# A third accumulating fold of the key totals, and a stack half as wide, in an attention kernel

## The chip, the cores and the metric

The kernel runs on one core of one Trainium2 chip. The metric is the device time of one execution in microseconds (us). Before the change it is 1807.54 us, the median of three runs (1806.34 to 1808.13).

## The reference

The input is 32 images of 256 channels on 32x32 pixels, in float32. Each image is group-normalized (32 groups of 8 channels), then goes through a causal self-attention with 8 heads of 32 dimensions over 1024 tokens, and the input is added to the output. A token attends only to tokens strictly before it:

```python
q = jnp.einsum('oc,bcs->bos', q_w, xf) + q_b[None, :, None]
kv = jnp.einsum('oc,bcs->bos', kv_w, xf) + kv_b[None, :, None]
...
mask = jnp.tril(jnp.ones((S, S), dtype=x.dtype), -int(MASK_CENTER))
scores = jnp.einsum('bhqd,bhkd->bhqk', q, k) / jnp.sqrt(jnp.asarray(dk, x.dtype))
scores = jnp.where(mask == 0, jnp.asarray(-10000.0, x.dtype), scores)
attn = jax.nn.softmax(scores, axis=-1)
attn = jnp.where(mask == 0, jnp.asarray(0.0, x.dtype), attn)
out = jnp.einsum('bhqk,bhkd->bhqd', attn, v)
...
x = x + _L0_conv_ref(_gn(x), q_w, q_b, kv_w, kv_b)
```

## The kernel before, in words

**Visits.** An image's attention is done in ten visits: two groups of four heads (g = 0, 1), and for each of them five visits (i = 0 to 4) that cover the lower triangle of keys by queries. In a visit TensorE makes transposed scores (keys on the partitions, queries along the row) for four heads: full blocks into two PSUM tiles `sT`, and triangular and odd pieces into one tile `tri`. ScalarE (ACT) takes their exponentials into SBUF tiles: `e` (128 keys x 4 heads x 512 queries) and `eh`. GpSimd (POOL) masks the triangular parts (`select`, L388), in place or into tiles `diagonal`. TensorE multiplies the exponentials with the values into a bank `acc`. The loop at L820 runs over all visits of all images; in its iteration i it writes down the scores of visit i, the values of visit i-1, and whatever the tables `at` and `after` hold for i. That fixes every engine's order by hand: five engines each work through their own list strictly in order, SyncE (SP) too, which issues most transfers.

**Key totals.** The softmax's denominators are sums of exponentials over all keys. VectorE (DVE) adds the visits' tiles together elementwise (`add_keys`, L490), so each image leaves four sums (two head groups by two query halves; n = 0 to 3 in the code), each a tile of 128 partitions x 4 heads x 512 queries, which still has to be summed over its 128 partitions. This is done by transfers: `fold` (L505) lets POOL issue an accumulating transfer that adds rows 64 to 127 onto rows 0 to 63 of the same tile, then another that adds rows 32 to 63 onto rows 0 to 31. Then `stack` (L511) lets SP copy the remaining 32 rows of each sum into 32 rows of one tile `folded`, so that the four sums lie above each other. `sum_folded` (L518, L519) transposes `folded` in 32x32 blocks, a head at a time, and reduces over the 32 keys: four transposes and four reductions per image, written into `rows`. `invert` (L547 to L559) checks the range, takes reciprocals and sends them to DRAM; `spread_inverses` (L573) reads them back, broadcast over 32 partitions each, into `rb`. `finish` (L598 to L607) multiplies, adds bias and input, and sends the output.

**The order around the change.** Sum n of image b is folded first at iteration first + SUMS[n] and second one iteration later; it is stacked at first + STACK[n], where first is the image's first visit. Both folds stand in POOL's list among the masks of the running visits; a fold waits there for the one before it to land, and POOL does nothing else meanwhile. The first fold of sum 1 also waits for a semaphore `begun`, which ACT raises at visit 7. In the same list stand, once an image, the gather of normalization statistics (`eight`, L212) and the small operations `rstd` and `shift` (L250, L254), for which ACT waits when it normalizes the next image (`xn`, L269). In SP's list a stack waits for the fold to land; `with_scores` (L568) holds some other issues until a given visit's scores have been made. The exponentials of visit 0 and 1 of each head group are written over the tiles of the same sums of the image before (four buffers `e0`), so they wait for those stacks.

The last image sums over keys on TensorE instead. The very first value projection, at the head of the program, uses the second half of a PSUM tile whose first half holds a projection of k.

Of the kernel before, what the change touches and what calls it, by code (L numbers as in the profile page):

```python
# [17 lines left out]
P = 128  # L18
# [10 lines left out]
ROW = 64  # L29
KEYS = 64  # L30
# [3 lines left out]
def tile_norm_attention_residual(  # L34
# [69 lines left out]
    def unshifted():  # L104
# [197 lines left out]
        def projections(b):  # L302

            def qk(n, g, hf, *bank):
                return lambda: project_qk(b, g, n, hf, *bank)

            def v(n, *bank):
                return lambda: project_v(b, n, *bank)

            early = [lone] if b == 0 else []  # L310
            return [
                qk(0, 0, 0, *early), qk(1, 0, 0), qk(0, 0, 1, *early), v(0), qk(1, 0, 1), qk(0, 1, 0, lone),
                qk(1, 1, 0), v(1), v(2), v(3), qk(0, 1, 1), qk(1, 1, 1, lone),
            ]
# [192 lines left out]
        def stack(b, n):  # L507
            if n == 0:
                live["folded", b] = work.tile([P, 4, HALF], F32, tag="folded", bufs=1, name=f"folded_{b}")
            total = live.pop(("sum", b, *divmod(n, NH)))  # L510
            nc.sync.dma_start(out=live["folded", b][n * HD : (n + 1) * HD], in_=total[:HD])  # L511

        def sum_folded(b, heads):
            if heads.start == 0:
                live["rows", b] = small.tile([P, ROW], F32, tag="rows", name=f"rows_{b}")
            for j in heads:
                turned = small.tile([P, HALF], F32, tag="turned", bufs=1, name=f"turned_{b}_{j}")
                nc.vector.transpose(turned, live["folded", b][:, j, :])  # L518
                nc.vector.tensor_reduce(  # L519
                    live["rows", b][:, j * HALF // HD : (j + 1) * HALF // HD],  # L520
                    turned.rearrange("p (k r) -> p k r", r=HD), AX.X, ALU.add,
                )
# [55 lines left out]
        def invert_here(b, n, within=slice(0, HALF)):  # L578


            if ("rb", b) not in live:
                live["rb", b] = work.tile([P, 4, HALF], F32, tag="folded", bufs=1, name="rb_last")
# [140 lines left out]
        STACK = (6, 9, 11, 14)  # L723
# [6 lines left out]
        with tc.manual_schedule(engines={ENG.PE, ENG.Activation, ENG.DVE, ENG.Pool, ENG.SP}):  # L730
# [14 lines left out]
            odd = work.tile([P, 4, HALF], F32, tag="folded", bufs=1, name="less_mean")[:, 0, :]  # L745
# [32 lines left out]
            for b in range(B):  # L778
# [14 lines left out]
                if not last:  # L793
                    for n in every:
# [3 lines left out]
                        when(first + STACK[n], lambda b=b, n=n: stack(b, n), at if n else after)  # L798
                    late = b == B - 2
                    v = first + N + (4 if late else 5)  # L800
# [215 lines left out]
```

## Time and profile before

| | us |
|---|---|
| median of the runs | 1807.54 |
| the profiled execution, its own time | 1806.47 |
| its span, from the first to the last instruction | 1803.3 |
| TensorE matmuls (PE) busy | 1782.8 |
| DVE busy | 1682.6 |
| ACT busy | 1469.8 |
| POOL busy | 833.2 |

The granted TensorE clock was 0.999 of full speed on average. A row of the timeline gives the start in us from the span's start, the duration in us, the engine, the line of the kernel, the operation, the tiles written and read, shapes and how many were merged into the row, and in brackets the idle time of the engine before it and what is thought to have ended it. A row of the waits gives engine and line, what was waited for, the total in us, how often, and the longest. A row of the transfers gives what is written and read, the issuing queue, the count, the size, and the median time from issue to landing in us. "Busy" of PE says that a matmul was under way, not that it ran at its best. The issue of a transfer on POOL is shown as an instruction of about 0.8 us; its landing comes later.

### The profile page before, as it was taken

Reading aid. Unit: us, or ns where it says so; the run is one execution under the profiler, and the core shown is the slowest. Engines: PE = TensorE matmul, PEld = TensorE weight load, DVE = VectorE, ACT = ScalarE, POOL = GpSimd, SP = SyncE. Lnnn points to the kernel's source line nnn. Section 1 sums busy time; section 2 is a strip of 40 time slices with the busy share of each in tenths; the row PEclk is TensorE's granted clock in tenths of the full one; section 3 lists DMA queues with packets and bytes.
Section 4 is the critical chain, followed back from the end, with each engine's and each line's share of the span. In section 5 each row is a group of like instructions: output and inputs, shape, how many; then the busy total and the mean of one; then the engine's idle time right before and its main releaser. Section 6 shows DMA issues by size and latency. Waiting matters only on the chain.

```text
span 1803.3 us, 82014 instructions
## 1 busy us (share of the span) xinstructions
PE 1782.8 (99%) x37208; PEld 983.7 (55%) x37208; DVE 1682.6 (93%) x1852; ACT 1469.8 (82%) x1736; POOL 833.2 (46%) x935
## 2 busy tenths in 40 slices
PE   8999999999999999999999999999999999999998
PEld 5555555555555555555555555555555555555554
DVE  3789999999999999999999999999999999999996
ACT  5888888888888888888888888888888888888884
POOL 2445644444444444544544444545444444445541
PEclk9999999999999999999999999999999999999999
DMA  2566776666766767767667666676676676666662
GB/s 69 105 118 129 150 134 137 137 138 136 149 127 138 144 134 148 129 134 143 131 145 146 129 137 142 137 148 128 136 147 131 145 143 131 138 140 136 131 120 86
DMA packets 92771, 240.23 MB, mean 133 GB/s; under 512 B 26272, under 2 KB 27792, under 8 KB 76544
## 3 DMA queue, kind: packets, MB, share of 16 engines
q0 software_dynamic: 17360, 100.58, 39.0%
q1 hardware_dynamic: 74912, 134.28, 26.3%
q8 instruction: 292, 4.78, 1.1%
q14 instruction: 63, 0.52, 0.1%
q10 hardware_dynamic: 144, 0.07, 0.0%
HBM read 69.90 MB, written 34.95 MB: 58 GB/s over the span
## 4 chain that ended last, share of the span: by engine, by line
PE 57%; DVE 32%; issue 5%; DMA 3%; ACT 2%; DVEq 0%; SPq 0%; POOL 0%; ACTq 0%
DVE e L490 20%; PE acc L472 17%; PE pp L180 14%; PE tri L381 10%; PE sT L381 8%; PE ppv L180 7%; DVE turned L518 3%; DVE rows L519 3%; DVE rb L601 2%; DMA rb<-inverses 2%; DVE num L598 2%; ACT eh L446 2%; DVE st L196 1%; PE pd L526 1%; DVE mv L219 1%
## 5 line engine op out<-in xcount | busy, mean ns | idle before, releaser
L443 ACT ACTIVATE e<-sT 128x1024 f32<-128x1024 f32 x640 | 620.8, 1022 | 209.1 <-PE sT L381 204.3
L381 PE MATMUL tri<-q,k 32*64 32x128 f32 (+4 forms) x12416 | 550.4, 298 | 8.8 <-ACT eh L446 8.1
L381 PE MATMUL sT<-q,k 32*64 32x256 f32 (+1 forms) x7424 | 548.7, 462 | 1.2 <-issue 1.2
L381 PEld LDWEIGHTS tri<-q,k 32*64 32x64 f32 x12416 | 389.0, 131 | 185.9 <-issue 86.6
L388 POOL TENSOR_SCALAR_AFFINE_SELECT diagonal<-eh 128x512 f32<-128x512 f32 x384 | 363.2, 966 | 265.6 <-ACT eh L446 265.3
L180 PE MATMUL pp<-xn,wT 128*32 128x512 f32 (+1 forms) x4224 | 477.5, 582 | 0.0
L490 DVE TENSOR_TENSOR e<-e,eh 128x1536 f32<-128x1536 f32 x375 | 438.3, 1169 | 41.5 <-PE acc L472 28.2
L446 ACT ACTIVATE eh<-tri 128x1536 f32<-128x1536 f32 (+1 forms) x320 | 453.2, 1416 | 23.6 <-DVE e L490 23.6
L490 DVE TENSOR_TENSOR e<-e,e 128x2048 f32<-128x2048 f32 x187 | 447.4, 2393 | 6.4
L505 POOL DMA_DIRECT2D e<-e x248 | 206.5, 833 | 414.9 <-DMA e<-e 360.9
L472 PE MATMUL acc<-e,v 128*32 128x512 f32 x2560 | 338.5, 600 | 1.1 <-POOL diagonal L388 1.1
L381 PEld LDWEIGHTS sT<-q,k 32*64 32x64 f32 x7424 | 301.1, 131 | 15.2 <-issue 1.9
L180 PEld LDWEIGHTS pp<-xn,wT 128*32 128x32 f32 x4224 | 140.5, 109 | 270.6 <-issue 216.2
L490 DVE TENSOR_TENSOR e<-e,diagonal 128x1024 f32<-128x1024 f32 x187 | 245.0, 1310 | 19.4
L180 PE MATMUL ppv<-wT,xn 128*32 128x256 f32 x4032 | 240.6, 379 | 0.0
L472 PE MATMUL acc<-eh,v 128*32 128x384 f32 (+3 forms) x3072 | 198.7, 346 | 0.0
L472 PEld LDWEIGHTS acc<-eh,v 128*32 128x32 f32 x3072 | 97.0, 110 | 143.1 <-issue 120.6
L180 PEld LDWEIGHTS ppv<-wT,xn 128*32 128x32 f32 x4032 | 129.7, 110 | 69.0
L388 POOL TENSOR_SCALAR_AFFINE_SELECT e<-e 128x512 f32<-128x512 f32 x64 | 73.2, 1144 | 196.1 <-ACT e L443 196.1
L269 ACT ACTIVATE xn<-x,shift,rstd 128x256 f32<-128x256 f32 x248 | 135.4, 594 | 8.8 <-POOL shift L254 8.4
L601 DVE SCALAR_TENSOR_TENSOR rb<-num,v_bias_col,x 128x256 f32<-128x256 f32 x248 | 131.3, 569 | 4.4
L472 PEld LDWEIGHTS acc<-e,v 128*32 128x32 f32 x2560 | 62.8, 108 | 105.2 <-issue 94.6
(94 smaller groups left out, 1267.9 us busy)
## 6 DMA issues: line engine op xcount, KB each, us to landing
e<-e POOLq DMA_DIRECT2D x124, 512.0 KB, 6.2
x<-in_x_dram SPq DMA_DIRECT2D x124, 256.0 KB, 4.1
e<-e POOLq DMA_DIRECT2D x124, 256.0 KB, 4.7
folded<-e SPq DMA_DIRECT2D x124, 256.0 KB, 4.5
rb<-inverses SPq DMA_DIRECT2D x124, 256.0 KB, 5.0
out_dram<-rb SPq DMA_DIRECT2D x124, 256.0 KB, 3.8
x<-in_x_dram SPq DMA_DIRECT2D x2, 512.0 KB, 5.8
inverses<-inv_turned SPq DMA_DIRECT2D x31, 32.0 KB, 2.9
```

What stands on the lines that cost most here:

```text
L180: nc.tensor.matmul(out[part, cols], lhsT=lhsT[:, part], rhs=rhs[:, cols], start=start, stop=stop, skip_group_check=True)
L269: nc.scalar.activation(to, of, AF.Identity, bias=live["shift", b][:, g : g + 1], scale=rstd)
L381: return nc.tensor.matmul(to[c : c + KEYS, at : at + width], lhsT=live["k", b, g][rows, kb * P + c : kb * P + c + KEYS], rhs=live["q", b, ...
L388: nc.gpsimd.affine_select(out=to, in_=of, pattern=[[0, 4], [(1, -1)[odd], P]], compare_op=ALU.is_gt, fill=0.0, base=0, channel_multiplier= ...
L443: nc.scalar.activation(e[:, heads[a][0] : heads[a][1] + 1 : step, :], banks[a], AF.Exp)
L446: exp = nc.scalar.activation(eh[:, :, :wide], tri.rearrange("p (j q) -> p j q", q=SHORT)[:, :, :wide], AF.Exp)
L472: nc.tensor.matmul(acc[HD * j : HD * (j + 1), of], lhsT=live["v", b][:, kb, h * HD : (h + 1) * HD], rhs=e[:, j, :], start=first, stop=last ...
L490: nc.vector.tensor_add(to, to, tile_of(b, g, at))
L505: nc.gpsimd.dma_start(out=total[:rows], in_=total[rows : 2 * rows], accum_op=ALU.add)
L518: nc.vector.transpose(turned, live["folded", b][:, j, :])
L519: nc.vector.tensor_reduce(live["rows", b][:, j * HALF // HD : (j + 1) * HALF // HD], turned.rearrange("p (k r) -> p k r", r=HD), AX.X, ALU ...
L601: nc.vector.scalar_tensor_tensor(blocks(rb, s), blocks(num, s, (start + s) % 2 == 1), v_bias_col[:, g : g + 1], blocks(xt[:, g, cols], s), ...
```

## The change

- **A third fold.** After the two folds, POOL issues a third accumulating transfer for each sum, which adds rows 16 to 31 onto rows 0 to 15. It stands one iteration after the second fold (SUMS[n] + 2).
- **A narrower stack.** The 16 rows that remain are stacked by two transfers, one for each half of the 512 queries, one under the other: `folded` becomes 128 partitions x 4 heads x 256 queries. Rows n·32 to n·32+15 hold the first half of sum n's queries, the next 16 rows the second half.
- **Half the operations on DVE.** `sum_folded` transposes two heads at once (2 x 256 columns) and reduces over 16 keys and not 32: two transposes and two reductions per image.
- **Places.** The stack of sum 0 moves from iteration 6 to 7, and to the end of the iteration. For the last but one image the sums over keys come one iteration later than before, as for the others.
- **Tiles.** Two tiles that shared the buffer of `folded` at the head and the end of the program go elsewhere or are taken as a slice of the smaller one.
- **The head.** The first value projection of image 0 uses the spare bank of the value products (`lone`).

```diff
+TURN = 16
...
-                qk(0, 0, 0, *early), qk(1, 0, 0), qk(0, 0, 1, *early), v(0), qk(1, 0, 1), qk(0, 1, 0, lone),
+                qk(0, 0, 0, *early), qk(1, 0, 0), qk(0, 0, 1, *early), v(0, *early), qk(1, 0, 1), qk(0, 1, 0, lone),
...
         def stack(b, n):
             if n == 0:
-                live["folded", b] = work.tile([P, 4, HALF], F32, tag="folded", bufs=1, name=f"folded_{b}")
+                live["folded", b] = work.tile([P, 4, HALFBANK], F32, tag="stacked", bufs=1, name=f"folded_{b}")
             total = live.pop(("sum", b, *divmod(n, NH)))
-            nc.sync.dma_start(out=live["folded", b][n * HD : (n + 1) * HD], in_=total[:HD])
+            for s in range(2):
+                at = n * HD + s * TURN
+                nc.sync.dma_start(
+                    out=live["folded", b][at : at + TURN], in_=total[:TURN, :, s * HALFBANK : (s + 1) * HALFBANK]
+                )

         def sum_folded(b, heads):
             if heads.start == 0:
                 live["rows", b] = small.tile([P, ROW], F32, tag="rows", name=f"rows_{b}")
-            for j in heads:
-                turned = small.tile([P, HALF], F32, tag="turned", bufs=1, name=f"turned_{b}_{j}")
-                nc.vector.transpose(turned, live["folded", b][:, j, :])
-                nc.vector.tensor_reduce(
-                    live["rows", b][:, j * HALF // HD : (j + 1) * HALF // HD],
-                    turned.rearrange("p (k r) -> p k r", r=HD), AX.X, ALU.add,
-                )
+            turned = small.tile([P, HALF], F32, tag="turned", bufs=1, name=f"turned_{b}_{heads.start}")
+            nc.vector.transpose(turned, live["folded", b][:, heads.start : heads.stop, :].rearrange("p j q -> p (j q)"))
+            nc.vector.tensor_reduce(
+                live["rows", b].rearrange("p (j s k) -> p j k s", s=2, k=HALFBANK // HD)[:, heads.start : heads.stop],
+                turned.rearrange("p (j k s r) -> p j k s r", j=len(heads), s=2, r=TURN), AX.X, ALU.add,
+            )
...
-        STACK = (6, 9, 11, 14)
+        STACK = (7, 9, 11, 14)
...
                         when(v + 1, lambda b=b, n=n: fold(b, n, HD), after)
-                        when(first + STACK[n], lambda b=b, n=n: stack(b, n), at if n else after)
+                        when(v + 2, lambda b=b, n=n: fold(b, n, TURN), after)
+                        when(first + STACK[n], lambda b=b, n=n: stack(b, n), after)
                     late = b == B - 2
-                    v = first + N + (4 if late else 5)
+                    v = first + N + 5
                     when(v, lambda b=b: sum_folded(b, every[:2]), after)
```

The three places where the order of instructions moves are these. First POOL, from visit 8 of one image to visit 1 of the next. In a name such as e_0_1_1265 the first number is the head group, the second the visit, the last a running number; a transfer e<-e is a fold, and 32x2048 in it says that it leaves 32 rows. Before:

```order
L505 DMA e_0_1_1265<-e_0_1_1265 32x2048
L388 AFFINE_SELECT diagonal_1_3_1925<-eh_1_3_1873 128x4x128 x2
L505 DMA e_1_0_1597<-e_1_0_1597 64x2048
L505 DMA e_1_0_1597<-e_1_0_1597 32x2048
L388 AFFINE_SELECT e_0_0_2034<-e_0_0_2034 128x4x128
L399 MEMSET e_0_0_2034 1x4
L388 AFFINE_SELECT eh_0_0_2035<-eh_0_0_2035 128x4x128
L212 DMA eight_2106<-each_2104,group_of 128x192
L388 AFFINE_SELECT diagonal_0_1_2147<-eh_0_1_2109 128x4x128 x2
```

And after the change:

```order
L506 DMA e_0_1_1271<-e_0_1_1271 32x2048
L389 AFFINE_SELECT diagonal_1_3_1930<-eh_1_3_1878 128x4x128 x2
L506 DMA e_0_1_1271<-e_0_1_1271 16x2048
L506 DMA e_1_0_1606<-e_1_0_1606 64x2048
L506 DMA e_1_0_1606<-e_1_0_1606 32x2048
L389 AFFINE_SELECT e_0_0_2041<-e_0_0_2041 128x4x128
L400 MEMSET e_0_0_2041 1x4
L389 AFFINE_SELECT eh_0_0_2042<-eh_0_0_2042 128x4x128
L506 DMA e_1_0_1606<-e_1_0_1606 16x2048
L213 DMA eight_2114<-each_2112,group_of 128x192
L389 AFFINE_SELECT diagonal_0_1_2155<-eh_0_1_2117 128x4x128 x2
```

The 16-row fold of sum 1 (e_0_1) now stands ahead of the 64-row fold of sum 2 (e_1_0), and the 16-row fold of sum 2 ahead of the gather `eight`.

Second SP, over the same stretch, from the inverses on. Before, with the stack of sum 0 at the top:

```order
L511 DMA folded_2619<-e_0_0_2034 32x2048
L559 DMA inverses_2698<-inv_turned_2696 128x2x32
L573 DMA rb_2796<-inverses_2698 32x4x512 x2
L511 DMA folded_2619<-e_0_1_2108 32x2048
L573 DMA rb_2796<-inverses_2698 32x4x512
L205 DMA each_2967<-st_2818 128x24
L573 DMA rb_2796<-inverses_2698 32x4x512
L511 DMA folded_2619<-e_1_0_2460 32x2048
```

And after the change:

```order
L563 DMA inverses_2702<-inv_turned_2700 128x2x32
L514 DMA folded_2736<-e_0_0_2041 16x4x256 x2
L577 DMA rb_2803<-inverses_2702 32x4x512 x2
L514 DMA folded_2736<-e_0_1_2116 16x4x256 x2
L577 DMA rb_2803<-inverses_2702 32x4x512
L206 DMA each_2977<-st_2826 128x24
L577 DMA rb_2803<-inverses_2702 32x4x512
L514 DMA folded_2736<-e_1_0_2471 16x4x256 x2
```

The inverses now stand ahead of the stack of sum 0, and every stack is two issues.

Third DVE, after the last addition of a round (L490), where the folded sums are reduced. Before:

```order
L518 STREAM_TRANSPOSE turned_0_2538<-folded_1756 128x512
L519 TENSOR_REDUCE rows_2537<-turned_0_2538 128x16
L518 STREAM_TRANSPOSE turned_1_2541<-folded_1756 128x512
L519 TENSOR_REDUCE rows_2537<-turned_1_2541 128x16
L518 STREAM_TRANSPOSE turned_2_2613<-folded_1756 128x512
L519 TENSOR_REDUCE rows_2537<-turned_2_2613 128x16
L518 STREAM_TRANSPOSE turned_3_2616<-folded_1756 128x512
L519 TENSOR_REDUCE rows_2537<-turned_3_2616 128x16
L547 SCALAR_TENSOR_TENSOR in_range<-rows_2537,in_range 128x64
```

And after the change:

```order
L522 STREAM_TRANSPOSE turned_0_2549<-folded_1871 128x512
L523 TENSOR_REDUCE rows_2548<-turned_0_2549 128x2x8x2
L522 STREAM_TRANSPOSE turned_2_2621<-folded_1871 128x512
L523 TENSOR_REDUCE rows_2548<-turned_2_2621 128x2x8x2
L551 SCALAR_TENSOR_TENSOR in_range<-rows_2548,in_range 128x64
```

Two transposes and two reductions are gone; all else on DVE stands as it did.

More of the change, by code (lines that the diff above doesn't have):

```diff
@@ L581, in invert_here @@
             if ("rb", b) not in live:
-                live["rb", b] = work.tile([P, 4, HALF], F32, tag="folded", bufs=1, name="rb_last")
+                live["rb", b] = xpool.tile([P, NG, S], F32, tag="x", name="rb_last").rearrange("p g (hf q) -> p (g hf) q", hf=NH)
             k = (within.stop - within.start) // HD
@@ L744, in unshifted @@
             keep_busy(6, HD)
-            odd = work.tile([P, 4, HALF], F32, tag="folded", bufs=1, name="less_mean")[:, 0, :]
+            odd = work.tile([P, 4, HALFBANK], F32, tag="stacked", bufs=1, name="less_mean").rearrange("p j q -> p (j q)")[:, :HALF]
             live["less_mean"] = odd.rearrange("p (g n t) -> p g n t", g=NG, t=P)
```

## The prediction

> **What bounds the kernel now.** I read the page first: busy shares say little here, because two engines look full.
>
> ```profile
> PE 1782.8 (99%) x37208; PEld 983.7 (55%) x37208; DVE 1682.6 (93%) x1852; ACT 1469.8 (82%) x1736; POOL 833.2 (46%) x935
> PE 57%; DVE 32%; issue 5%; DMA 3%; ACT 2%; DVEq 0%; SPq 0%; POOL 0%; ACTq 0%
> ```
>
> So I took the period of an image from the timeline of ACT: the exponential of the triangular part of visit 0, at images 2, 3, 15, 16 and 31.
>
> ```profile
> 135.17 1.46 ACT L446 ACTIVATE eh<-tri 128x1536 f32<-128x1536 f32 x1
> 189.66 1.45 ACT L446 ACTIVATE eh<-tri 128x1536 f32<-128x1536 f32 x1
> 853.21 1.46 ACT L446 ACTIVATE eh<-tri 128x1536 f32<-128x1536 f32 x1
> 908.53 1.46 ACT L446 ACTIVATE eh<-tri 128x1536 f32<-128x1536 f32 x1
> 1736.67 1.45 ACT L446 ACTIVATE eh<-tri 128x1536 f32<-128x1536 f32 x1
> ```
>
> From image 2 to image 31 are 29 images in 1601.5 us, 55.22 each; 15 to 16 takes 55.32. Image 2, when little finishing work had yet come to DVE, took 54.49. That is TensorE's own pace; the other 0.73 us are lost once an image, and the waits and timelines say where:
>
> ```profile
> ACT eh L446 <- DVE e L490: 23.6, 28, 1.4
> 889.16 0.70 DVE L518 STREAM_TRANSPOSE turned<-folded 128x512 f32<-128x512 f32 x1
> 894.29 0.69 DVE L519 TENSOR_REDUCE rows<-turned 128x16 f32<-128x512 f32 x1
> 896.17 2.56 DVE L490 TENSOR_TENSOR e<-e,eh 128x1536 f32<-128x1536 f32 x2
> 898.02 1.45 ACT L446 ACTIVATE eh<-tri 128x1536 f32<-128x1536 f32 x1 [0.84 <-DVE e L490]
> ```
>
> The eight transposes and reductions stand from 889.16 to 894.98, 5.82 us in one piece; the add behind them frees an eh buffer late, and visit 8's exponential waits 0.84 us for it. DVE bounds the period by that much. But POOL, at 46%, is no free engine: it works in order and sits in waits for its own transfers, and one of its results is already only just in time.
>
> ```profile
> POOL e L505 <- DMA e<-e: 360.9, 91, 8.4
> ACT xn L269 <- POOL shift L254: 8.4, 18, 1.2
> ```
>
> The timeline of POOL over one round shows the chain (sum 1's 64-row fold is the one held back for `begun`, raised at visit 7; the cause printed there is a guess):
>
> ```profile
> 891.36 0.85 POOL L505 DMA_DIRECT2D e<-e  x1 [1.63 <-DVE turned L518]
> 898.37 0.80 POOL L505 DMA_DIRECT2D e<-e  x1 [3.46 <-DMA e<-e]
> 899.56 2.29 POOL L388 TENSOR_SCALAR_AFFINE_SELECT diagonal<-eh 128x512 f32<-128x512 f32 x2 [0.39 <-ACT eh L446]
> 901.80 0.84 POOL L505 DMA_DIRECT2D e<-e  x1
> 909.83 0.79 POOL L505 DMA_DIRECT2D e<-e  x1 [7.18 <-DMA e<-e]
> 910.34 0.93 POOL L388 TENSOR_SCALAR_AFFINE_SELECT e<-e 128x512 f32<-128x512 f32 x1
> 911.38 2.01 POOL L388 TENSOR_SCALAR_AFFINE_SELECT eh<-eh 128x512 f32<-128x512 f32 x1
> 914.89 1.62 POOL L212 DMA_INDIRECT eight<-each,group_of  x1 [1.50 <-DMA each<-st]
> 916.52 1.87 POOL L388 TENSOR_SCALAR_AFFINE_SELECT diagonal<-eh 128x512 f32<-128x512 f32 x2
> 918.34 0.91 POOL L505 DMA_DIRECT2D e<-e  x1
> 925.00 0.81 POOL L505 DMA_DIRECT2D e<-e  x1 [2.20 <-DMA e<-e]
> 925.57 1.56 POOL L250 TENSOR_TENSOR rstd<-rstd,power 128x2 f32<-128x2 f32 x1
> 927.21 0.20 POOL L254 TENSOR_TENSOR shift<-mean,rstd 128x2 f32<-128x2 f32 x1
> 927.44 1.09 ACT L269 ACTIVATE xn<-x,shift,rstd 128x256 f32<-128x256 f32 x2 [0.40 <-POOL shift L254]
> 928.64 1.94 ACT L443 ACTIVATE e<-sT 128x1024 f32<-128x1024 f32 x2
> ```
>
> From `begun` at 891.36 to the normalization (xn) at 927.44 are 36.08 us, and the exponentials of visit 4 follow it 0.11 us after its end. From there to the next `begun`, 55.32 us after the last, are 19.24 us. This is a ring, and it closes within a few tenths of the period: whatever lengthens its POOL part lengthens the image.
>
> **The change part by part.** *Removed from DVE:* two of four transposes and two of four reductions an image, half of 5.82 us or 2.91. The new ones handle as many elements (128x512) each, so I take their old 0.70 and 0.69 us; the reduction now has an output of 32 in place of 16, and even at twice its time 1.5 us are saved. That is more than the 0.84 us of visit 8's wait. Beyond that wait DVE's slack is worth nothing, as TensorE's 54.49 us come next: the gain ends at 0.73 us an image, 29 times 21 us.
>
> *Added to POOL:* a 16-row fold of 128 KB for each of four sums, in order and behind a wait for the 32-row fold of the same sum. What such a wait lasts, SyncE shows, which stacks sum 1 as soon as that fold has landed, and ACT and the page give the neighbours:
>
> ```profile
> 903.23 0.52 SPq L511 DMA_DIRECT2D folded<-e  x1
> 912.08 1.94 ACT L443 ACTIVATE e<-sT 128x1024 f32<-128x1024 f32 x2 [0.52 <-PE sT L381]
> e<-e POOLq DMA_DIRECT2D x124, 512.0 KB, 6.2
> e<-e POOLq DMA_DIRECT2D x124, 256.0 KB, 4.7
> folded<-e SPq DMA_DIRECT2D x124, 256.0 KB, 4.5
> ```
>
> 903.23 less 898.37 is 4.86 us from issue to use. I keep it, and 0.80 us for the issue. Then, with the rows above:
> - Sum 1's 16 rows go out at 903.23, where POOL has been done with the selections since 901.85. Sum 2's 64 rows follow at 904.03, not 901.80: 2.23 us late.
> - Its 32 rows waited 8.03 us before (901.80 to 909.83), where the two other sums of this stretch waited 7.01 (891.36 to 898.37) and 6.66 (918.34 to 925.00). The long one had SyncE's 256 KB stack beside it, which now comes later and is half as large; I take 7.01: 911.04.
> - The selections (910.34 to 913.39 before) fit into the next wait. Sum 2's 16 rows go at 911.04 + 4.86 = 915.90, and the gather of the statistics, queued behind, at 916.70 and not 914.89: 1.81 us late. With 6.66 it is 1.46, with 8.03 it is 2.83. The gather's old wait for SyncE's transfer of statistics is covered by this.
> - From the gather on nothing is added before xn, so `shift` is 1.81 us late as well. Some of that may come back: see the 1.01 us of rstd below, where POOL ran late, against 1.56 here. I take off those 0.55.
>
> Sum 0's 16 rows fall into POOL's idle time ahead of `begun` and sum 3's into its wait for visit 5; I cost both at nothing. If that cover is missing, each costs up to 0.8 us of issue in the same ring.
>
> The ring becomes 36.08 + 1.81 - 0.55 + 19.24, less the 0.11 us that ACT had left: 56.47 us an image against 55.22, 1.25 more. Its low end, with 6.66 us and the selections at 916.52 also done in 1.22 instead of 1.87, is 55.47; its high end, with 8.03 and nothing recovered, 58.04.
>
> That POOL's lateness does reach ACT and TensorE, one image of before shows. A slow transfer had moved sum 2's 32 rows to 2.88 us after visit 0's exponential (1.30 in the round above):
>
> ```profile
> 410.52 1.46 ACT L446 ACTIVATE eh<-tri 128x1536 f32<-128x1536 f32 x1
> 413.40 0.76 POOL L505 DMA_DIRECT2D e<-e  x1 [8.43 <-DMA e<-e]
> 414.68 1.94 ACT L443 ACTIVATE e<-sT 128x1024 f32<-128x1024 f32 x2 [1.14 <-PE sT L381]
> 428.73 1.01 POOL L250 TENSOR_TENSOR rstd<-rstd,power 128x2 f32<-128x2 f32 x1
> ```
>
> Visit 1's exponentials then waited 1.14 us for TensorE and not 0.52: the values of visit 0 stood behind POOL's mask, and 0.62 us were lost at once.
>
> *Moved on SyncE:* the stack of sum 0 goes behind the inverses, the others wait for a third landing, and each is two issues (0.52 us apiece). Behind the stack of sum 1 stand the spread of inverses, the statistics and the last spread. Between 256 KB in 4.7 us and 512 KB in 6.2 lie 1.5 us, so 128 KB should land in about 4.0 (an estimate from those two rows): the stack starts near 907.3, not 903.23, and its second half lands, by the 4.5 us of the old one at most, by 912.4. ACT's exponential of visit 1 in the next image overwrites that buffer and would run at 912.08, or 0.84 earlier without visit 8's stall: up to 1.1 us of waiting. But this is upstream of xn's wait in the same round, and ACT loses the larger of the two, not both; I add nothing. The Trainium skill ("DMA: Bandwidth & Descriptors", Anatomy of one DMA) fits a software DMA as 2.0 us plus its bytes over 436e3 per us, 3.2 us for 512 KB and 2.6 for 256. The rows here, 6.2 and 4.7, disagree, and decide; with its times all four chains would end early, and the sum would be rival 1's.
>
> *Head and tail, once:* the first value projection takes the spare bank. The waits for k there are in the waits of the page
>
> ```profile
> PEld pp L180 <- ACT k L283: 3.4, 2, 1.7
> ```
>
> so between 0 and 1.7 us are saved; I take 1. For image 30 the sums stand one visit later; DVE has idle time in the last image, I take 0, at most 3 us.
>
> Sum: 29 x 1.25 = 36, less 1: 1806.47 us of the profiled execution becomes about 1841. Its own time lies 1.1 us below the median of the runs, so I say 1842.
>
> **The rivals.**
> 1. *The third folds fit, TensorE is the bound.* For it: POOL idles half the time, and nothing forces the long waits if transfers land sooner with less on the queues. Against: the shortest waits of this round (6.66 and 4.86) already give 55.47. It decides if POOL's part of the ring is under 35.3 us. Worth 29 x 0.73 + 1 = 22 us: about 1784.
> 2. *What DVE gives, POOL takes back:* the ring at its low end or just under, 55.1 to 55.3 an image, 1803 to 1809.
> 3. *Transfers collide.* DVE is done 2.91 us sooner, so the inverses and two spreads of 256 KB go out sooner too, beside sum 1's 32-row fold, whose landing now sits in the ring; before, they ran beside the long 8.03. Then that is paid elsewhere and the ring is 57.5 to 58.04: 29 x 2.3 to 2.8 us, 1873 to 1888. For it: 8.03 against 6.66 shows that the company matters. Against: sum 3's fold at 918.34 has an output transfer beside it and waits 6.66 us all the same:
>
> ```profile
> 919.15 9.72 SPq L607 DMA_DIRECT2D out_dram<-rb  x3
> ```
>
> The Trainium skill says that software and hardware queues take turns inside each DMA engine (same page, SWDGE vs HWDGE vs iDMA); the trace's 8.03 agrees with that.
>
> **How the numbers follow.** The forecast, slower by 7 to 60 us, gets 0.58, rival 3 gets 0.17, rival 2 gets 0.07, rival 1, with all between 1784 and 1803, 0.18. A change of 0.2%, 3.6 us, is about what a measurement of this kernel can tell: slower 0.75, same 0.07, faster 0.18. The forecast's own range is 1813 to 1868. The whole range runs from 1794, inside rival 1, to 1878, inside rival 3.
>
> **What would show it.** In the changed profile: DVE's L490 no longer in ACT's waits for eh, and DVE waiting for others (right for DVE's part); the fold line with 372 issues and much more than 360.9 us of idle time before them; ACT's xn waiting for `shift` in nearly every image, over 1 us each; period 56 to 57 us. If xn's wait is gone and the period is 54.5, the ring was misjudged: the waits for folds were shorter than their rows of before. If ACT waits for stacks at visit 1 instead, the place is wrong and the sign right.

## The result, and the profile after

The changed kernel takes 1891.81 us (median of six runs, 1881.54 to 1896.02). Beside it the kernel before takes 1807.04, so the ratio is 1.0459, with a 95% interval of 1.0431 to 1.0487. It is slower, as forecast, but by 85 us where 35 were forecast, and it lies above the end of the range, 1878. The profiled execution took 1892.62 us, its span is 1890.9.

The page after, busy times and shares of the chain that ended last:

```profile
PE 1809.5 (96%) x37208; PEld 990.7 (52%) x37208; DVE 1560.4 (83%) x1728; ACT 1467.4 (78%) x1736; POOL 901.0 (48%) x1059
PE 57%; issue 11%; DMA 11%; DVE 8%; POOL 6%; ACT 6%; POOLq 1%; SPq 1%; ACTq 0%; DVEq 0%
```

DVE lost 122 us of work, and its share of the chain fell from 32% to 8%. "issue", DMA, POOL and ACT together rose from 10% to 34%: the end is now set by many short waits in turn. The same two rows of ACT's timeline as before, images 2 and 31:

```profile
135.25 1.46 ACT L447 ACTIVATE eh<-tri 128x1536 f32<-128x1536 f32 x1
1818.41 1.46 ACT L447 ACTIVATE eh<-tri 128x1536 f32<-128x1536 f32 x1
```

An image takes 1683.16 / 29 = 58.04 us, not 55.22. The 2.82 us more make 82 of the 88 us by which the span grew; the rest, 5.9 us, lies behind image 31's first visit (72.5 us to the end, against 66.6). Nothing came in ahead of image 2.

The waits after, in us in total, how many, and the longest:

```profile
POOL e L506 <- DMA e<-e: 464.6, 162, 7.8
ACT e L444 <- DMA folded<-e: 94.4, 34, 6.0
ACT xn L270 <- POOL shift L255: 9.4, 24, 0.8
```

and the page's group of folds, and its transfers (number, size, median us from issue to landing):

```profile
L506 POOL DMA_DIRECT2D e<-e x372 | 309.9, 885 | 587.7 <-DMA e<-e 464.6
...
e<-e POOLq DMA_DIRECT2D x124, 512.0 KB, 7.0
...
e<-e POOLq DMA_DIRECT2D x124, 256.0 KB, 4.8
...
e<-e POOLq DMA_DIRECT2D x124, 128.0 KB, 4.2
folded<-e SPq DMA_DIRECT2D x248, 64.0 KB, 4.4
```

The wait of xn for `shift`, where the prediction looked for the loss, is about what it was (9.4 us, and 8.4 before). What grew is the wait of ACT's exponentials for the stack: they overwrite a buffer that SyncE is still reading. And the 64-row folds land in 7.0 us where they took 6.2. The chain of one image, from POOL's, SyncE's and ACT's timelines (924.50 is sum 0's 16-row fold, 926.00 sum 1's 64 rows, 933.33 its 32 rows, 938.59 its 16 rows and sum 2's 64, 942.89 its two stacks, 947.90 the exponentials of visit 1):

```profile
924.50 0.81 POOL L506 DMA_DIRECT2D e<-e  x1 [0.50 <-DMA x<-in_x_dram]
926.00 0.81 POOL L506 DMA_DIRECT2D e<-e  x1 [0.69 <-DVE turned L522]
...
933.33 0.81 POOL L506 DMA_DIRECT2D e<-e  x1 [2.49 <-issue]
...
938.59 1.66 POOL L506 DMA_DIRECT2D e<-e  x2 [2.40 <-DMA e<-e]
```

```profile
942.89 1.33 SPq L514 DMA_DIRECT2D folded<-e  x2
```

```profile
942.20 1.46 ACT L447 ACTIVATE eh<-tri 128x1536 f32<-128x1536 f32 x1
...
947.90 1.94 ACT L444 ACTIVATE e<-sT 128x1024 f32<-128x1024 f32 x2 [2.67 <-DMA folded<-e]
```

From `begun` to visit 1's exponentials are 21.90 us here; in the round that the prediction quotes they were 20.72 (891.36 to 912.08). In the median of images 4 to 27 they are 22.52 against 20.90, worked out from the starts in the two traces. The first exponential of visit 0 to that of visit 1 takes 8.12 us (median) in place of 5.37; no other step of the ten grew by over 0.64, and the step from visit 7 to 8, where DVE's stall was, fell from 6.00 to 4.92.

### The profile page after: what moved, and what is told of

Same layout as the page of the kernel before. It is cut to its first block, busy times and chain, and to the rows that moved or that the text cites. A ratio compares the mean times of both kernels' runs of the same rounds, so it can differ in the third digit from the quotient of the medians.

```text
span 1890.9 us, 82491 instructions
## 1 busy us (share of the span) xinstructions
PE 1809.5 (96%) x37208; PEld 990.7 (52%) x37208; DVE 1560.4 (83%) x1728; ACT 1467.4 (78%) x1736; POOL 901.0 (48%) x1059
## 4 chain that ended last, share of the span: by engine, by line
PE 57%; issue 11%; DMA 11%; DVE 8%; POOL 6%; ACT 6%; POOLq 1%; SPq 1%; ACTq 0%; DVEq 0%
PE acc L473 18%; PE pp L181 12%; PE tri L382 10%; PE sT L382 9%; PE ppv L181 8%; DVE e L491 5%; DMA e<-e 5%; DMA folded<-e 4%; POOL diagonal L389 4%; ACT e L444 3%; POOL e L506 2%; ACT eh L447 2%; POOLq L503 1%; DMA eight<-each,group_of 1%; ACT q L284 1%
## 5 line engine op out<-in xcount | busy, mean ns | idle before, releaser
L506 POOL DMA_DIRECT2D e<-e x372 | 309.9, 885 | 587.7 <-DMA e<-e 464.6
L382 PE MATMUL sT<-q,k 32*64 32x256 f32 (+1 forms) x7424 | 564.0, 462 | 0.9 <-issue 0.3
L181 PE MATMUL pp<-xn,wT 128*32 128x512 f32 (+1 forms) x4224 | 491.8, 589 | 43.1 <-ACT e L444 42.9
L389 POOL TENSOR_SCALAR_AFFINE_SELECT diagonal<-eh 128x512 f32<-128x512 f32 x384 | 375.2, 1008 | 208.8 <-ACT eh L447 208.5
L491 DVE TENSOR_TENSOR e<-e,eh 128x1536 f32<-128x1536 f32 x375 | 427.2, 1139 | 46.1 <-PE acc L473 32.6
L491 DVE TENSOR_TENSOR e<-e,e 128x2048 f32<-128x2048 f32 x187 | 431.3, 2306 | 6.4
L473 PE MATMUL acc<-e,v 128*32 128x512 f32 x2560 | 345.1, 601 | 22.7 <-ACT q L284 18.5
L491 DVE TENSOR_TENSOR e<-e,diagonal 128x1024 f32<-128x1024 f32 x187 | 250.7, 1341 | 20.1 <-DVE e L491 0.9
L602 DVE TENSOR_TENSOR num<-num,rb 128x512 f32<-128x512 f32 x124 | 87.9, 709 | 89.0 <-DMA rb<-inverses 89.0
L220 DVE BATCH_NORM_AGGREGATE mv<-eight 128x2 f32<-128x96 f32 x62 | 32.1, 560 | 131.5 <-DMA eight<-each,group_of 131.5
```

The lines of the kernel that those rows point to most:

```text
L181: nc.tensor.matmul(out[part, cols], lhsT=lhsT[:, part], rhs=rhs[:, cols], start=start, stop=stop, skip_group_check=True)
L220: nc.vector.bn_aggr(live["mv", b][:, g, :], live["eight", b][:, :, g, :])
L382: return nc.tensor.matmul(to[c : c + KEYS, at : at + width], lhsT=live["k", b, g][rows, kb * P + c : kb * P + c + KEYS], rhs=live["q", b, ...
L389: nc.gpsimd.affine_select(out=to, in_=of, pattern=[[0, 4], [(1, -1)[odd], P]], compare_op=ALU.is_gt, fill=0.0, base=0, channel_multiplier= ...
L473: nc.tensor.matmul(acc[HD * j : HD * (j + 1), of], lhsT=live["v", b][:, kb, h * HD : (h + 1) * HD], rhs=e[:, j, :], start=first, stop=last ...
L491: nc.vector.tensor_add(to, to, tile_of(b, g, at))
```

## The experiments

Two theories stood at the start. Theory 1: what costs is the folds, as waits and issues in POOL's ordered list, and ACT or TensorE feel it wherever the ring happens to close. Theory 2: what costs is one thing beside them, such as the place of the stacks, the collision of transfers, or the traffic. In each experiment the period is that of images 2 to 31, from the two exponentials as above.

**VectorE's part alone.** The changed kernel without third folds:

```diff
-                        when(v + 2, lambda b=b, n=n: fold(b, n, TURN), after)
```

> The changed kernel without the third fold: 16 of the 32 rows that remain are stacked, and the other 16 are left out of the sums. It has DVE's gain and the narrow stacks, and POOL's list is that of before. Theory (POOL's waits for folds lengthen the ring, DVE's gain itself is real): a period of 54.5 us, no wait of ACT for DVE at visit 8, about 1784 us. Rival (the earlier spreads of inverses, which DVE's gain brings, collide with the folds): the folds of sums 1 and 2 land later than before here too, and the time is above 1807 us.

Measured: 1786.27 us, ratio 0.9889 (0.9869 to 0.9909). Its images 2 and 31 on ACT:

```profile
133.94 1.46 ACT L447 ACTIVATE eh<-tri 128x1536 f32<-128x1536 f32 x1
1719.22 1.46 ACT L447 ACTIVATE eh<-tri 128x1536 f32<-128x1536 f32 x1
```

The period is 54.66 us, and 54.48 or 54.49 in 25 of these 29 images: TensorE's pace. VectorE's gain is worth 20 us, its inverses and spreads go out earlier here (the first spread 3.2 us ahead of sum 1's 32-row fold, in the kernel before 1.2 us behind it, in the median of images 4 to 27), and nothing collides that costs time. So the third folds cost 106 us, 1786 to 1892.

**The folds alone.** The kernel before with a third fold for each sum, and VectorE's work unchanged:

```diff
-        STACK = (6, 9, 11, 14)
+        STACK = (7, 9, 11, 14)
...
-                        when(first + STACK[n], lambda b=b, n=n: stack(b, n), at if n else after)
+                        when(v + 2, lambda b=b, n=n: fold(b, n, HD // 2), after)
+                        when(first + STACK[n], lambda b=b, n=n: stack(b, n), after)
```

> The kernel before with the third fold added and the stack moved as in the change, but 32 rows stacked in one transfer and DVE's eight operations kept; rows 16 to 31 are counted twice in the sums. Theory: the folds alone make the loss, a period of 57 to 58 us, 1860 to 1890 us. Rival (the loss comes with DVE's earlier spreads or with two issues for each stack): under 1840 us.

Measured: 1920.29 us, ratio 1.0631 (1.0591 to 1.0671), more than any theory had. The folds make the loss without VectorE's part. Why it is larger than in the changed kernel is not shown: VectorE's gain, 20 us by itself, may hide some of it there, but TensorE's granted clock also fell to half in 11 of this kernel's 29 images, for 44 us in all, and in four of the changed kernel's, for 14.

**Is it the wait for the stack?** The changed kernel with a fifth buffer for the totals, so that visit 1 writes where no stack reads; the space comes from the last image's denominators, which go to a free tile of x.

```diff
-            e = epool.tile([P, 4, HALF], F32, tag="e0" if i < 2 else "e", bufs=4 if i < 2 else 3, name=f"e_{name}")
+            e = epool.tile([P, 4, HALF], F32, tag="e0" if i < 2 else "e", bufs=5 if i < 2 else 3, name=f"e_{name}")
```

> The changed kernel with five buffers for the exponentials that become sums (room for it comes from three tiles of the last image, which go elsewhere), so that the exponentials of visit 1 no longer wait for the stack of sum 1. If that wait alone bounds the period (58.0 us): it falls to about 55, 1800 us. If the chain over the gather and the normalization is nearly as long, as its last wait of 0.26 us at xn says: about 57.3 us, 1870 us, with ACT's waits for the normalization's shift grown from 9.4 us to 20 or more.

Measured: 1919.50 us, ratio 1.0627 (1.0578 to 1.0675). Both numbers were missed. Its waits:

```profile
POOL e L506 <- DMA e<-e: 592.9, 176, 7.8
PEld acc L473 <- POOL e L400: 70.9, 26, 4.3
ACT xn L270 <- POOL shift L255: 57.8, 30, 2.9
```

The wait for the stack is gone from ACT's list, and the period grew to 59.31 us. TensorE now waits for POOL's mask of visit 0 (L400 ends it), and xn for `shift`. Eleven of the images have a stretch at half the clock here too, but the other 18 still take 58.6 us on average, where the 25 images of the changed kernel without such a stretch take 57.75. So the wait for the stack was where the loss was felt, not what made it. That it had held ACT back, and POOL had so been less late at the next places, is a reading and was not tested by itself.

**A later third fold.** With five buffers, each third fold goes behind the next sum's 64-row fold, so that POOL doesn't stand waiting for the 32-row fold just issued:

```diff
-        STACK = (7, 9, 11, 14)
+        STACK = (8, 11, 12, 14)
+        THIRD_AT = (6, 8, 11, 14)
...
-                        when(v + 2, lambda b=b, n=n: fold(b, n, TURN), after)
+                    for n in every:
+                        when(first + THIRD_AT[n], lambda b=b, n=n: fold(b, n, TURN), after)
```

> Five buffers as well, and each third fold stands behind the next sum's 64-row fold, where POOL waits anyway; the stacks of sums 0, 1 and 2 stand one or two visits later on SyncE. Theory (what costs is that POOL stands in a wait of its own for each third fold): the waits are gone, TensorE bounds, 54.5 to 55 us a period, 1784 to 1800 us, faster than before. Rival (the third folds cost by the traffic that they add, or by queueing ahead of the next folds): 1820 us or more.

Measured: 1828.83 us, ratio 1.0122 (1.0077 to 1.0168); period 55.97, where 17 of the 29 images take under 55.3 us and eight take 57 to 61.3. The same folds and bytes in another order cost 43 us against the kernel without third folds, where they cost 106 in the changed kernel and 133 in the one with five buffers. So the order, of the folds on POOL with the stacks later on SyncE, is most of the price. It is not all of it: the time lies in the range of the rival, 1820 us or more, by which the third folds cost something even where POOL doesn't wait for them by themselves. In one slow image POOL's and SyncE's timelines read:

```profile
576.32 1.73 POOL L506 DMA_DIRECT2D e<-e  x2 [1.21 <-issue]
587.13 0.81 POOL L506 DMA_DIRECT2D e<-e  x1 [7.29 <-issue]
```

```profile
569.00 1.24 SPq L514 DMA_DIRECT2D folded<-e  x2
570.34 2.87 SPq L613 DMA_DIRECT2D out_dram<-rb  x1
573.32 3.57 SPq L114 DMA_DIRECT2D x<-in_x_dram  x4
```

The first of the two folds, sum 1's 64 rows, landed 9.5 us after it went out, beside the loads of x that follow the stack and the output; the next fold of POOL waited for it. That suggested the next run, with the last stack behind those loads:

```diff
-        STACK = (8, 11, 12, 14)
+        STACK = (8, 11, 12, 15)
```

> As the late third folds with five buffers (1829 us), but SyncE stacks sum 3 one visit later, behind the loads of the next image. In the slow images of that run the loads came 3 us late behind that stack and ran beside the 64-row fold of sum 1, which then took 9.6 us to land; most other images took 54.5 us. If that meeting makes them slow: few such images remain, 1785 to 1805 us, faster than before. If the slow images come from the third folds' own queueing: 1820 to 1835 us, no change.

Measured: 1848.29 us, ratio 1.0251 (1.0201 to 1.0302). The loads do go out earlier there, and no 64-row fold of sum 1 whose landing the trace has takes more than 7.3 us from image 2 on. The kernel got slower all the same, so that explanation of the slow images fell, and what makes them is open.

**Is it the traffic?** The changed kernel with thin third folds, 256 bytes a row in place of 8 KB:

```diff
+            if rows == TURN:
+                nc.gpsimd.dma_start(
+                    out=total[:rows, 0, :KEYS], in_=total[rows : 2 * rows, 0, :KEYS], accum_op=ALU.add
+                )
```

> The changed kernel in which each third fold adds only 64 columns of one head (256 bytes a row in place of 8 KB); what it leaves out is missing from the sums. POOL's list, its waits and issues are as in the change, nearly all the traffic of the third folds is gone. Theory 1 (the waits and issues in POOL's list make the loss): the period stays near 57.5, at least 1860 us. Theory 2 (a 64-row fold lands later, 7.0 us by the median in place of 6.2, because it is queued right behind a 16-row fold's 8 KB rows): 64-row folds land in 6.2 us again, the period falls by 1 to 2 us, 1830 to 1860 us.

Measured: 1890.94 us, ratio 1.0462 (1.0407 to 1.0516), as slow as with full ones. Its waits and its transfers:

```profile
ACT xn L270 <- POOL shift L255: 98.4, 29, 5.7
ACT e L444 <- DMA folded<-e: 15.8, 13, 3.1
```

```profile
e<-e POOLq DMA_DIRECT2D x124, 512.0 KB, 5.9
...
e<-e POOLq DMA_DIRECT2D x124, 4.0 KB, 2.0
```

By the totals the bytes cost nothing. The 64-row folds land in 5.9 us again (the trace has 15 of these landings), the exponentials hardly wait for stacks, and xn waits 29 times for `shift`, 3.4 us each: this is the place that the prediction named, reached with a fold that moves next to nothing.

But the totals hide a second effect. Many images take about 56 us here and many about 60.5, and what parts them is a wait of TensorE and its granted clock behind it. Where xn is late, TensorE stands idle for 2 to 4 us, and in 14 of the 29 images the clock then fell to half, for 3.4 or 6.8 us. One of these places, first TensorE's timeline and then the busy times of the stretch, where 0.50 is the granted clock:

```profile
805.51 2.85 PE L181 MATMUL ppv<-wT,xn 128*32 128x256 f32 x32 [2.96 <-ACT e L444]
```

```profile
806.40:809.80 3.40, 3.40 (x54) 2.17 (x54) 3.19 (x3) 2.70 (x4) 0.43 (x1) 0.50 0.83 134
```

The 14 images take 60.65 us on average, the other 15 take 56.32. In the changed kernel the 25 images at full clock take 57.75. Half of the 64.9 us at half clock, at most 32 us, is an estimate of what the clock costs here; in the changed kernel, with 13.7 us, it is at most 7. So the two equal totals don't show that the bytes are free. What is shown is that thin folds cost as well: even the images at full clock take 1.7 us more than those without third folds (54.66), and that much is not the bytes'. How the rest divides between bytes and list is open. One more difference between the traces is the 64-row wait of sum 3, which stands right ahead of `shift` on POOL: 7.21 us here, 5.88 in the changed kernel (medians of images 4 to 27); what makes it longer was not tested.

**Which sums?** The third fold for some of the sums only, with a condition ahead of that line, `if n in (1, 2):`, `if n in (0, 3):`, `if n != 3:` and `if n != 0:`.

> The changed kernel with third folds for sums 1 and 2 alone; sums 0 and 3 lose the 16 rows that are not folded. The prediction took the third folds of 0 and 3 to be free: then this is as slow as the change, 1870 to 1895 us. If each third fold costs about the same, half the loss against the kernel without any (1786 us) is left: about 1838 us.

> The changed kernel with third folds for sums 0 and 3 alone, sums 1 and 2 losing 16 rows. If those two are free, as the prediction took them to be: 1786 to 1792 us, a period of 54.5 us. If every third fold costs alike: about 1838 us.

> The changed kernel with third folds for sums 0, 1 and 2 only; of sum 3, 16 of the 32 rows are stacked and the other 16 are left out. Known so far: no third fold 1786, sums 0 and 3 alone 1799, sums 1 and 2 alone 1833, all four 1892; 46 us of the last figure belong to neither pair alone. Theory A (sum 0's third fold stands right ahead of sum 1's 64-row fold in POOL's order, so it pushes the part of the ring that sums 1 and 2 lengthen): most of the 59 us between 1833 and 1892 come with sum 0: 1865 to 1892. Theory B (sum 3's third fold, ahead of sum 0's 64 rows, pushes the whole list): 1833 to 1845. Theory C (each of the four takes some slack, and the list has none left only with all of them): about 1855 to 1865 here and in the next kernel alike.

> The changed kernel with third folds for sums 1, 2 and 3 only; of sum 0, 16 of the 32 rows are stacked and the other 16 are left out. Theory A: 1833 to 1850. Theory B: 1865 to 1892. Theory C: about 1855 to 1865.

Measured, with the two ends:

| third folds | us | ratio to before | period, us |
|---|---|---|---|
| none | 1786.27 | 0.9889 (0.9869 to 0.9909) | 54.66 |
| sums 0, 3 | 1798.74 | 0.9947 (0.9930 to 0.9965) | 54.96 |
| sums 1, 2 | 1833.21 | 1.0142 (1.0118 to 1.0166) | 56.15 |
| sums 0, 1, 2 | 1863.00 | 1.0329 (1.0308 to 1.0350) | 57.13 |
| sums 1, 2, 3 | 1862.29 | 1.0311 (1.0295 to 1.0326) | 57.28 |
| all | 1891.81 | 1.0459 (1.0431 to 1.0487) | 58.04 |

Sums 0 and 3 cost 12 us by themselves and 59 us once 1 and 2 are there, 30 and 29 of them with either one. That is what Theory C of the expectations had: while the ring has slack they lie in it, and when the ring sets the period each is paid.

For sum 0 the traces show how. POOL's timeline with sums 1 and 2 only (565.10 is sum 1's 64-row fold, 571.64 its 32 rows, 577.18 its 16 rows and sum 2's 64):

```profile
565.10 0.85 POOL L506 DMA_DIRECT2D e<-e  x1 [1.77 <-DVE turned L522]
571.64 0.80 POOL L506 DMA_DIRECT2D e<-e  x1 [1.49 <-issue]
577.18 1.66 POOL L506 DMA_DIRECT2D e<-e  x2 [1.68 <-DMA e<-e]
```

and with sums 0, 1 and 2, where sum 0's 16 rows (515.03) go out right ahead of sum 1's 64:

```profile
515.03 0.80 POOL L506 DMA_DIRECT2D e<-e  x1
516.14 0.82 POOL L506 DMA_DIRECT2D e<-e  x1 [0.31 <-DVE rows L523]
524.25 0.82 POOL L506 DMA_DIRECT2D e<-e  x1 [3.06 <-issue]
529.77 1.66 POOL L506 DMA_DIRECT2D e<-e  x2 [2.43 <-DMA e<-e]
```

The second fold follows sum 1's first by 8.11 us in place of 6.54. The medians of images 4 to 27 are 7.78 and 6.87, with the 64 rows landing in 6.75 and 5.64 us; from `begun` to visit 1's exponentials it becomes 22.44 in place of 21.30 us, and the period 57.13 in place of 56.15. With sums 0 and 3 alone the 64 rows land as late (6.97 in the nine of these images whose landing the trace has, 7.98 to the second fold), and the median image takes 54.54 all the same: there the chain isn't the ring. For sum 3 no such step was found: its typical image is 0.4 us longer (56.55 against 56.13) and five images of 59 to 62 us, three of them with a stretch at half the clock, make the rest of its mean.

**VectorE's gain without POOL.** What remained open was how a complete kernel can have the 20 us. In the first attempt no sum is folded a third time: its 32 rows are stacked half as wide in two layers of 16, and VectorE adds the layers.

```diff
+            for a in range(2):
+                for s in range(2):
+                    at = n * HD + s * TURN
+                    nc.sync.dma_start(
+                        out=live["folded", b][at : at + TURN, a],
+                        in_=total[a * TURN : (a + 1) * TURN, :, s * HALFBANK : (s + 1) * HALFBANK],
+                    )
...
+            folded = live["folded", b][:, :, heads.start : heads.stop, :]
+            nc.vector.tensor_add(folded[:, 0], folded[:, 0], folded[:, 1])
```

> A complete kernel without any third fold: each sum's 32 rows are stacked half as wide in two layers of 16 rows, by four transfers of SyncE, and VectorE adds the layers before it transposes and reduces. VectorE: two adds of 128x512 more an image than in the kernel without third folds, an estimate of 0.7 us each from the 0.69 us of the reduction of as many elements; of the 2.91 us saved 1.5 are left, more than the 0.84 us that visit 8 waited before. If POOL's third folds are what the change pays and VectorE's gain is worth what it seemed, 1786 to 1792. If the two more issues of SyncE for each sum (0.52 us apiece) or the adds bring a wait back, 1795 to 1810.

Measured: 1802.20 us, ratio 0.9967 (0.9954 to 0.9980). Lines from its groups, and POOL's and SyncE's timelines in one of its longer images (512.63 is sum 2's 64 rows, 516.07 the four stacks of sum 1, 523.21 sum 2's 32 rows):

```profile
L524 DVE TENSOR_TENSOR folded<-folded 128x512 f32<-128x512 f32 x62 | 53.1, 856 | 3.8 <-DMA out_dram<-rb 3.8
```

```profile
512.63 0.85 POOL L506 DMA_DIRECT2D e<-e  x1
523.21 0.77 POOL L506 DMA_DIRECT2D e<-e  x1 [9.73 <-DMA folded<-e]
```

```profile
516.07 3.87 SPq L515 DMA_DIRECT2D folded<-e  x4
```

An add takes 0.86 us, so 1.2 us of the 2.91 are left, enough for the 0.84 of visit 8; but the four stacks run beside POOL's fold, and POOL waits 10.58 us from one fold to the next. With the stacks back at their old places in SyncE's order,

```diff
-        STACK = (7, 9, 11, 14)
+        STACK = (6, 9, 11, 14)
...
-                        when(first + STACK[n], lambda b=b, n=n: stack(b, n), after)
+                        when(first + STACK[n], lambda b=b, n=n: stack(b, n), at if n else after)
```

> The complete kernel with two layers added on VectorE, the stacks back at the places in SyncE's order that they had before the change. If the place of the stacks behind the inverses and beside sum 2's 64-row fold (that fold landed in 10.3 us in one image beside four stack transfers of sum 1, against 7 to 8) makes the upsets, 1786 to 1795; if the number of transfers does, wherever they stand, 1798 to 1804 as with the stacks later; if sum 0's stack ahead of the inverses now makes these late, above 1804.

it took 1798.55 us, ratio 0.9960 (0.9944 to 0.9976). That interval overlaps the one above, so the place moved little; the number of transfers is left as the likelier cause, argued from these two runs and not tested by itself.

The last run leaves POOL and SyncE as they were before the change, and lets VectorE take two heads in one instruction:

```diff
-            for j in heads:
-                turned = small.tile([P, HALF], F32, tag="turned", bufs=1, name=f"turned_{b}_{j}")
-                nc.vector.transpose(turned, live["folded", b][:, j, :])
...
+            turned = small.tile([P, len(heads) * HALF], F32, tag="turned2", bufs=1, name=f"turned_{b}_{heads.start}")
+            nc.vector.transpose(turned, live["folded", b][:, heads.start : heads.stop, :].rearrange("p j q -> p (j q)"))
```

> A complete kernel: before, with two heads transposed and reduced at a time, so that VectorE has two transposes and two reductions of 128x1024 an image in place of four and four of 128x512; nothing is changed on POOL and SyncE, and no fold is added. By the reductions and transposes of before (0.69 and 0.71 us) and the smallest transpose in the trace (0.245 us for 128x64) an instruction has an estimated 0.18 us that do not depend on its size; four fewer are 0.7 us an image. If VectorE's lateness in visit 8 is what bounds before and POOL and SyncE are not touched, most of 0.73 us an image come back: 1786 to 1795. If lumps twice as long hold up the adds as before, 1800 to 1807.

Measured: 1797.62 us, ratio 0.9955 (0.9943 to 0.9968). Its groups, and ACT's wait that was 23.6 us before:

```profile
L517 DVE STREAM_TRANSPOSE turned<-folded 128x1024 f32<-128x1024 f32 x62 | 76.8, 1239 | 2.6 <-DMA folded<-e 1.5
L518 DVE TENSOR_REDUCE rows<-turned 128x32 f32<-128x1024 f32 x62 | 75.6, 1220 | 2.1
```

```profile
ACT eh L446 <- DVE e L490: 11.0, 22, 0.9
```

Two transposes and two reductions take 4.92 us by these means, where four and four took 5.58 (0.708 and 0.686 us each, the means of before): 0.66 us less, and a little over half of ACT's wait goes with it. The period is 54.90 us. The time lies between the two ranges that were expected: part of the 20 us came back, not most of it. That is a smaller saving on VectorE than the change's, and the kernel is 94 us faster than the changed one, and 0.45% faster than before. None of these three kernels has the whole 20 us.

## Why the prediction was right in part, and where it was wrong

- **DVE bounds by 0.73 us an image, worth at most 21 us: right.** Alone it gave 20 us (1806 to 1786), and the image takes TensorE's 54.49 us. The new reduction takes 0.69 us, as assumed.
- **The ring through POOL turns the gain into a loss: right in sign and mechanism.** Its sum, 56.47 us, priced the third folds of sums 1 and 2 and no others. A kernel with just these has 56.15 us and takes 1833 us, against the 1841 of that sum. How near it came is in part luck. There the gather comes 2.6 us later behind `begun` than in the kernel before (26.41 against 23.77, medians of images 4 to 27), where 1.81 was priced, more of it is made up before `shift` (36.66 against 35.70, 1.0 us later, where 1.26 was priced), and ACT's waits are shared between `shift` (31.0 us in all) and the stack (38.3), to which the sum gave nothing.
- **"Sum 0's 16 rows fall into POOL's idle time ahead of `begun` and sum 3's into its wait for visit 5; I cost both at nothing": this is the step that failed.** They cost 59 us, more than the 50 us by which the forecast missed. The cover that the prediction named is there as long as the ring has slack (12 us for both). The price given for its loss, up to 0.8 us of issue each, was near but still too low: 0.98 and 1.13 us an image (57.13 and 57.28 against 56.15). For sum 0 it isn't the issue; a 64-row fold that goes out just over 1 us behind a 16-row fold lands 1.1 us later, and that fold begins the ring. For sum 3 the way it costs stays open.
- **The durations.** In the changed kernel sum 1's 64-row wait was taken at 7.01 us and is 8.17 in the median of images 4 to 27; sum 2's was taken at 7.01 too and is 7.59; sum 1's 32-row wait was 4.86 and is 5.29; a 16-row fold was estimated to land in 4.0 us and lands in 4.2. The first has the largest error: in the kernel before, the last fold ahead of it goes out 7.5 us earlier (median), and now one goes out 0.7 us earlier.
- **"The stack ... up to 1.1 us of waiting ... I add nothing": the place was wrong, as the last sentence of the prediction allowed.** With the waits that it took, the stack would have landed 21.0 us behind `begun`; the exponentials came 22.5 behind it, and this chain became the longer of the two. ACT waits 2.8 us a time there (94.4 in 34 waits), and xn hardly more than before. Where it waits is not what it pays: without that wait the kernel was slower still (1920), and with thin folds the loss sat at xn (1891).
- **Rival 3 gave the nearest number and not the cause.** The meeting that it named is there: the first two spreads go out 0.9 and 0.5 us ahead of sum 1's 32-row fold, where before they followed it by 1.2 and 1.6 (medians of images 4 to 27). But the fold lands in 5.0 us in place of 4.7, which is 0.3 us and not the 1.0 to 1.6 that the rival needs above 56.47, and the kernel with sums 1 and 2 alone has the same meeting (0.8 and 0.4 us ahead) at 56.15 us an image. The high end of the ring, 58.04, was met to the hundredth by luck: the 8.03 us that made it are 7.59 now. Rivals 1 and 2 fell with the result: nothing of the gain is left.
- **Head and tail.** The first exponential of image 0 comes 0.98 us earlier (21.21 to 20.23), as the 1 us said, but image 2 has none of it left. One trace of each doesn't show the 1 us: in the kernels with the new head this start lies between 19.71 and 22.46. The tail, taken at 0 to 3 us, costs 5.9. Without third folds it is 66.5 us long, as before (66.6), so the folds lengthen it and not the later place of the sums.
- **The rule on software DMA.** The Trainium skill ("DMA: Bandwidth & Descriptors", Anatomy of one DMA) has 2.0 us plus the bytes over 436e3. The thin fold of 4 KB lands in 2.0 us, which agrees; the accumulating folds of 128, 256 and 512 KB land in 4.2, 4.8 and 7.0 us, where it has 2.3, 2.6 and 3.2. For their part that grows with size, the rows decide.

## What to carry to other kernels

When an engine works through a list in order and waits there for its own transfers, price every entry that a change adds, also those that today fall into idle time: the idle time is the ring's slack, and it is one stock for all of them. Here the entries of sums 0 and 3 cost 12 us as long as the stock was there, and 59 when those of sums 1 and 2 had used it up. A wait that shows after a change is where the ring closes, not what lengthened it; take it away and see whether the period falls. Before two totals are held against each other, read the granted clock of both: a wait that leaves TensorE idle can be followed by matmuls at half the pace. And before work is moved from a busy engine to one that "idles half the time", look whether the busy one can do it in fewer, larger instructions: that gave 0.45% here, with nothing moved.

## What the runs showed of the hardware that was not expected

- An accumulating fold of 512 KB (sum 1's) lands in 5.6 us with no other fold right ahead of it, and in 6.7 when one of 128 KB went out on the same queue 1.2 us earlier (medians, images 4 to 27, of the kernels with third folds of sums 1, 2 and 0, 1, 2). Behind one of 4 KB it takes 5.5 to 6.0, but the trace has only four of these landings.
- In the kernel with thin folds TensorE's granted clock fell to half in 14 of 29 images. Each such stretch of 3.4 or 6.8 us began during an idle time of TensorE of 2.2 to 4.2 us or within 1.1 us of its end; idle times of 1.7, 2.4 and 2.6 us passed without one. The 32 matmuls of the value projection (`ppv<-wT,xn`) that follow took 1.56 us from the first start to the last at the full clock, and 3.01 where they fell wholly into such a stretch.
- On VectorE, twice the elements cost 1.75 to 1.78 times the time: 708 to 1239 ns for the transpose and 686 to 1220 ns for the reduction, 128x512 to 128x1024 in float32. By these two points 0.18 and 0.15 us of an instruction don't depend on its size, an estimate.
- Loads of x (256 KB) took 7.2 us to land in the kernel with five buffers, against 4.1 before and 4.7 in the changed kernel; why was not tested.
